# Attention and feed-forward: next keys begun inside the queries, weights loaded over the last tokens, router product on DVE, output stored by GpSimd

## The chip, the cores and the metric

One core of a Trainium2 chip runs the whole program. The metric is the device time of one execution in microseconds (us). Of the kernel before there are three timed executions and one profiled execution; the profile is of one execution alone.

## What is computed

The input is a batch of 4 images, 256 channels of 56 x 56 points, in fp32. Layer 0 is an involution: a group norm, then for each point and each of 32 groups of channels a softmax over a 7 x 7 window, worked out from the window itself, weighs that window; its result is added to the image. Layer 1 takes the 3136 points of an image as tokens of 256 values:

```python
t = _to_tokens(x)
t = t + _L1_attn_ref(_ln_t(t), ...)
t = t + _L1_ffn_ref(_ln_t(t), ...)
x = _from_tokens(t, x)
```

The attention has 8 heads of 32 and no exponential: its weights are a square, divided by their sum over the keys.

```python
scores = jnp.einsum('bnhd,bmhd->bhnm', q, k) * scale
t = jnp.square(scores + C_SHIFT)
attn = t / jnp.sum(t, axis=-1, keepdims=True)
out = jnp.einsum('bhnm,bmhd->bnhd', attn, v).reshape(B, N, D)
return out @ proj_w.T + proj_b
```

The feed-forward works only on the half of the tokens whose router weight is largest, and adds its result, times that weight, to their own rows:

```python
weights = (jnp.einsum('bsd,do->bso', x, wr) + br)[..., 0]
...
_, idx = jax.lax.top_k(weights, k)
sel_idx = idx[:, :kk]
...
h = jax.nn.gelu(jnp.einsum('bkd,dh->bkh', sel, w1) + b1)
y = jnp.einsum('bkh,hd->bkd', h, w2) + b2
...
y = y * w_sel[..., None]
```

## The kernel before

Two functions do the work, one after the other. `conv_layer` computes layer 0 and ends at about 1875 us of the span; the change doesn't touch it. `attn_ffn_layers` (L860) does the rest.

**Attention as sums over pairs.** Since the weights are squares of inner products, the sum over the keys is taken first: for each head, the products of all pairs of the 32 entries of a key, times v, are summed over the tokens, and each query then needs only its own products of pairs. So an image b has two passes, each for two groups g of four heads:

- `keys(b, g)` (L1021) goes over 25 blocks m of 128 tokens. `tokens(m)` issues the projection on PE (matmuls pv) and hands it to ACT and POOL (ls); `features(m)` multiplies the pairs on DVE (phi, 128 x 1920); `add(m, phi)` sums them on PE (accs, accq), one block behind. `coefficients` (L1101) turns the sums into coefficients.
- `queries(b)` (L1222) goes over 7 chunks q of 448 tokens, two groups g and four blocks k of pairs: matmuls pg, a square on ACT (ph), and on PE, one block behind, `add` (acc). After the last block the result is copied by DVE (av).

**Side work.** Everything else is put into a list, `later` (L1416 and on: `aside` at L1473, `run` at L1476). Each entry is a generator; `run` steps the main pass, and after each of its yields `aside` steps every entry once. A yield is therefore a unit of delay, "an aside" below. The side work of the queries is:

- `weigh(b, q, g)` (L1198), the sums by which to divide: matmul pu, on DVE dd, one yield, matmul pn, on DVE dn.
- `divide` (L1279): dn to another layout by four loads on SP (inv), an add and a reciprocal on DVE, a round trip through DRAM on SP (flat, rec), av times rec on DVE; for g = 1 then `tokens_out`.
- `tokens_out(b, q)` (L1313): the output projection on PE (po), added to the tokens on DVE (tk, two buffers), statistics and normalisation on DVE (the rows, which the feed-forward gathers later), uw = rows x router weights and tk + rows on POOL, and two yields later the reduce of uw to w on DVE, and the store of tk into the output on SP.
- `normalise(b + 1, q)` (L975), the layer norm of the next image's tokens, into xn, of which there is one; and `project(b, q + 1)` (L1181), the next chunk's queries (pq).
- `select(b)` (L1376), after the last chunk: the top half of the image's tokens by a search on the bits of w, and then 28 indirect DMAs on POOL, two to a yield, that scatter the rows into `us[b]` in DRAM. For images 0 to 2 it is put into the queries of the next image, for image 3 into the feed-forward.

**The order.** Every instruction of this function is issued through `InOrder` (L841), which keeps each engine's instructions in the order in which the program issues them. So all of them are recorded at L849, and the profile is read by the names of the tiles. An engine whose next instruction waits does nothing else; this holds for the DMA queues of SP and of POOL too.

**The feed-forward** (from L1497) begins after `inner.close()`, which gives back the buffers of the attention, xn among them. Then the loads of w1, w2 (1 MB each) and b2 are issued, and `fetch(0)` and `fetch(1)`, which load rows of `us`. There are 16 parts, four to an image, of 4, 4, 4 and 2 blocks of 112 tokens. For each: `turn` (L1518, transposes ft on PE), `first` (L1532, matmuls ph and a gelu on ACT), `second` (L1551, matmuls py, the rest on DVE (fz, fy), and indirect DMAs on POOL that write the rows into the output), and the `fetch` of the part after next.

The lines on which the side work of an output chunk ends:

```python
gp.tensor_tensor(uw, u, wr.to_broadcast([TB, 4, C]), ALU.mult)
gp.tensor_tensor(tk, tk, u, ALU.add)
yield
yield
w = held["w", b][:, q * 4 : q * 4 + 4]
ve.tensor_reduce(w, uw, AX.X, ALU.add)
...
sy.dma_start(
    out[b, q * CH : (q + 1) * CH].rearrange("(j p) c -> p j c", p=TB), tk
)
```

Of the kernel before, what the change touches and what calls it, by code (L numbers as in the profile page):

```python
# [7 lines left out]
F32 = mybir.dt.float32  # L8
I32 = mybir.dt.int32
AF = mybir.ActivationFunctionType  # L10
ALU = mybir.AluOpType
# [4 lines left out]
P = 128  # L16
NB = 4
C = 256
# [14 lines left out]
FF = 4 * C  # L33
TOPK = int(0.5 * HW) - 1
CH = 8 * W
NCH = HW // CH
NT = (HW + P - 1) // P
TB = 112
NTB = HW // TB
ROW_N = C + 4  # L40
# [821 lines left out]
def attn_ffn_layers(  # L862
# [27 lines left out]
    outp = ctx.enter_context(tc.tile_pool(name="attn_out", bufs=2))  # L890
    tkp = ctx.enter_context(tc.tile_pool(name="tokens", bufs=2))
    slp = ctx.enter_context(tc.tile_pool(name="select", bufs=1))
    mm = ctx.enter_context(tc.tile_pool(name="attn_mm", bufs=2, space=PSUM))
    accp = ctx.enter_context(tc.tile_pool(name="attn_acc", bufs=2, space=PSUM))
    sm = ctx.enter_context(tc.tile_pool(name="attn_sm", bufs=2, space=PSUM))

    inner = ctx.enter_context(ExitStack())
    xnp = inner.enter_context(tc.tile_pool(name="xn", bufs=1))
    kp = inner.enter_context(tc.tile_pool(name="k", bufs=3))
    php = inner.enter_context(tc.tile_pool(name="phi", bufs=2))  # L900
    cp = inner.enter_context(tc.tile_pool(name="coef", bufs=2))
# [2 lines left out]
    ve, te, se, sy, gp = (  # L904
        InOrder(tc, e) for e in (nc.vector, nc.tensor, nc.scalar, nc.sync, nc.gpsimd)
    )
# [35 lines left out]
    p = sm.tile([P, 512], F32, tag="sm", name="pvb")  # L942
# [77 lines left out]

    def keys(b, g):  # L1021

        accs = accp.tile([P, 512], F32, tag="acc", name=f"accs_{b}_{g}")
        accq = accp.tile([P, 512], F32, tag="acc", name=f"accq_{b}_{g}")
        held["sums", b, g] = accs, accq
        vs, ks = {}, {}
        size = lambda m: min(P, HW - m * P)

        def tokens(m):

            mn = size(m)
            if m % 2 == 0:
                held["kv"] = mm.tile([P, 2, 512], F32, tag="mm", name=f"pv_{b}_{g}_{m}")
            p = held["kv"][:mn, m % 2]
            for c in range(2):
                te.matmul(
                    p[:, : 2 * P], xn[:, c, m * P : m * P + mn],
                    wqkv[:, c, C:].rearrange("p (i o) -> p i o", i=2)[:, :, g * P : (g + 1) * P],
                    start=c == 0, stop=c == 1,
                )  # L1040
            k = ks[m] = p[:, :P].rearrange("p (h e) -> p h e", e=DH)
            se.activation(
                lss[m % NKV][:mn, :, HALF : HALF + 2 * DH].rearrange("p h (i e) -> p h i e", i=2),
                k.unsqueeze(2).to_broadcast([mn, 4, 2, DH]), AF.Identity,
            )
            v = vs[m] = kp.tile([P, P], F32, tag="v", name=f"v_{b}_{g}_{m}", bufs=5)
            se.activation(v[:mn], p[:, P : 2 * P], AF.Identity)

        def features(m):

            mn = size(m)
            ls, k = lss[m % NKV], ks.pop(m)
            phi = php.tile([P, 4, NF], F32, tag="phi", name=f"phi_{b}_{g}_{m}")
            mine = ls[:mn, :, HALF : HALF + DH]
            se.activation(phi[:mn, :, :DH], mine, AF.Square)
            ve.tensor_tensor(
                phi[:mn, :, DH:].rearrange("p h (l e) -> p h l e", e=DH),
                k.unsqueeze(2).to_broadcast([mn, 4, HALF - 1, DH]),
                further(ls[:mn, :, HALF + 1 : HALF + 1 + DH], HALF - 1), ALU.mult,
            )  # L1060
            gp.tensor_tensor(
                ls[:mn, :, :HALF], mine[:, :, :HALF], mine[:, :, HALF:], ALU.mult
            )
            return phi

        def add(m, phi):
            mn = size(m)
            v, ls = vs.pop(m), lss[m % NKV]
            first, last = m == 0, m == NT - 1
            for h, r in enumerate(QUARTERS):  # L1070
                te.matmul(accs[r], v[:mn, r], phi[:mn, h], start=first, stop=last)
            for h, r in enumerate(QUARTERS):
                te.matmul(
                    accq[r, :LS], v[:mn, r], ls[:mn, h], start=first, stop=last,
                    skip_group_check=True,
                )

            for h, r in enumerate(QUARTERS):
                k = ls[:mn, h, HALF:]
                te.matmul(  # L1080
                    accq[r, P : P + LS - HALF], k[:, :DH], k, start=False, stop=last,
                    skip_group_check=True,
                )

        tokens(0)
        tokens(1)
        yield
        tokens(2)
        yield
        waiting = None  # L1090
        for m in range(NT):
            phi = features(m)
            if waiting:
                add(*waiting)
            waiting = m, phi
            if m + 3 < NT:
                tokens(m + 3)
            yield
        add(*waiting)
# [98 lines left out]
    def weigh(b, q, g):  # L1198

        gram, line = held["form", b, g]  # L1200
        qT = held["q", b, q][0]
        p = sm.tile([P, 512], F32, tag="sm", name=f"pu_{b}_{q}_{g}")
        te.matmul(
            p[:, :CH], gram, qT[:, g], start=True, stop=True
        )
        dd = qp.tile([P, CH], F32, tag="dd", name=f"dd_{b}_{q}_{g}", bufs=1)
        ve.scalar_tensor_tensor(dd, p[:, :CH], line, qT[:, g], ALU.add, ALU.mult)
        yield

        n = CH // 4  # L1210
        p = sm.tile([P, 512], F32, tag="sm", name=f"pn_{b}_{q}_{g}")
        for j, r in enumerate(QUARTERS):
            te.matmul(
                p[r, :n], heads, dd[:, j * n : (j + 1) * n], start=True, stop=True,
                skip_group_check=True,
            )
        dn = outp.tile([P, n], F32, tag="dn", name=f"dn_{b}_{q}_{g}", bufs=3)
        ve.tensor_copy(dn, p[:, :n])
        held["dn", b, q, g] = dn
        yield  # L1220

    def queries(b):  # L1222
# [26 lines left out]
        for q in range(NCH):  # L1249
            for g in range(2):  # L1250
# [2 lines left out]
                    later.append(normalise(b + 1, q))  # L1253
                if g == 1 and q + 1 < NCH:
                    later.append(project(b, q + 1))
                for k in range(FB):
                    qT = held["q", b, q][0]
                    p = [
# [15 lines left out]
                        add(*waiting)  # L1274
                    waiting = q, g, k, phi
                    yield
        add(*waiting)

    def divide(b, q, g, av):  # L1279
# [33 lines left out]
    def tokens_out(b, q, both):  # L1313

        t = load(b, q, "tr")
        if q == 0:
            held["rows", b] = (slp if b % 2 else xnp).tile(
                [TB, NTB, ROW_N], F32, tag="rows", name=f"rows_{b}"
            )
            held["w", b] = slp.tile([TB, NTB], F32, tag="w", name=f"w_{b}", bufs=2)  # L1320
# [34 lines left out]
        for j in range(4):  # L1355
# [4 lines left out]
        ve.tensor_copy(rows[:, :, C + 2], mv[:, :, 0])  # L1360
        ve.tensor_scalar(rows[:, :, C + 3], dev, 1.0, None, ALU.add)
        uw = tkp.tile([TB, 4, C], F32, tag="uw", name=f"uw_{b}_{q}", bufs=1)
        gp.tensor_tensor(uw, u, wr.to_broadcast([TB, 4, C]), ALU.mult)
        gp.tensor_tensor(tk, tk, u, ALU.add)
        yield
        yield
        w = held["w", b][:, q * 4 : q * 4 + 4]
        ve.tensor_reduce(w, uw, AX.X, ALU.add)
        ve.tensor_scalar(w, w, col("br")[:TB], None, ALU.add)
        sy.dma_start(  # L1370
            out[b, q * CH : (q + 1) * CH].rearrange("(j p) c -> p j c", p=TB), tk
        )
        if q == NCH - 1:
            (later if b == NB - 1 else whole).append(select(b))

# [100 lines left out]
    def run(steps):  # L1476
        for _ in steps:
            aside()
# [3 lines left out]
    for q in range(NCH):  # L1482
        f = slice(q * CH, (q + 1) * CH)
        sy.dma_start(xn[:, :, f], ln0.rearrange("(c p) f -> p c f", p=P)[:, :, f])
    for b in range(NB):
        for g in range(2):
            run(keys(b, g))
            later.append(coefficients(b, g))
            aside()
            if g == 0:  # L1490
                later.append(project(b, 0))
        later.extend(whole)
        whole.clear()
        run(queries(b))

    inner.close()
    fp = ctx.enter_context(tc.tile_pool(name="ffn", bufs=2))  # L1497
    w1 = fp.tile([P, 2, FF], F32, name="w1", bufs=1)
    sy.dma_start(w1, d["ffn_w1"].rearrange("(c p) o -> p c o", p=P))
    w2 = fp.tile([P, FF // P, C], F32, name="w2", bufs=1)  # L1500
    sy.dma_start(w2, d["ffn_w2"].rearrange("(c p) o -> p c o", p=P))
    b2 = fp.tile([TB, 1, C], F32, name="b2", bufs=1)
    sy.dma_start(b2[:, 0], d["ffn_b2"].unsqueeze(0).to_broadcast([TB, C]))

    blocks = (TOPK + TB - 1) // TB
    parts = [(b, m, min(4, blocks - m)) for b in range(NB) for m in range(0, blocks, 4)]

    def fetch(i):


        b, m, k = parts[i]
        rows = fp.tile([TB, 4, ROW_N], F32, tag="rows", name=f"frows_{i}", bufs=3)
        sy.dma_start(
            rows[:, :k], us[b][m * TB : (m + k) * TB].rearrange("(j p) c -> p j c", p=TB)
        )
        held["part", i] = rows

    def turn(i):  # L1518
        k = parts[i][2]
# [64 lines left out]
                )  # L1584
            yield

    fetch(0)
    fetch(1)
    for i in range(len(parts) + 1):
        if i < len(parts):  # L1590
            turn(i)
# [160 lines left out]
```

## Time and profile before

| what | value |
| --- | --- |
| median of three runs | 3934.23 us (3933.35 to 3941.9) |
| the profiled execution's own time | 3942.82 us |
| its span | 3940.7 us |
| mean clock granted to TensorE | 0.959 |
| busy, PE / DVE / ACT / POOL | 3537.7 / 2609.8 / 1945.4 / 1812.5 us |
| start and end of image 0's keys, queries | 1882 - 2040, 2040 - 2263 us |
| image 1 | 2263 - 2430, 2430 - 2704 us |
| image 2 | 2704 - 2860, 2860 - 3142 us |
| image 3 | 3142 - 3290, 3290 - 3514 us |
| feed-forward | 3514 - 3941 us |

How to read it: the page gives each engine's busy time, the span in 40 slices with the busy tenths of each engine, the chain of work that ended last, and groups of instructions by tile. The trace behind it can be asked for waits (which engine waited at which tile for which other engine's tile, how long in total, how often, and the longest) and for a timeline (start, duration, engine, instruction, shapes; in brackets the idle time of the engine just before it and what ended it). A name such as `uw<-rows,awr` is the instruction's output and inputs. DMAs are named in the same way: `us<-rows,to` is a scatter of rows into `us`. A transfer's queue is SPq where SP issued it.

### The profile page before, as it was taken

What the parts mean: (1) busy time and instruction counts of PE and PEld (TensorE: products, weight loads), DVE (VectorE), ACT (ScalarE), POOL (GpSimd) and SP (SyncE); (2) the same over time, 40 slices, a digit from 0 to 9 for tenths busy, and PEclk for the clock granted to TensorE, in tenths of its full rate; (3) what the DMA queues carried; (4) which work ended last, traced back from release to release, by engine and by line L of the source; (5) the groups of instructions that cost most, each with busy time, mean ns of one, the idle gap of its engine ahead of it and who ended that gap; (6) DMA issues with size and microseconds to landing.
All of it is one profiled execution on the core that took longest, in us unless ns stands there. A gap on an engine that the chain in (4) does not pass through costs nothing.

```text
span 3940.7 us, 61459 instructions
## 1 busy us (share of the span) xinstructions
PE 3537.7 (90%) x23248; PEld 1595.4 (40%) x23248; DVE 2609.8 (66%) x3411; ACT 1945.4 (49%) x4093; POOL 1812.5 (46%) x1000
## 2 busy tenths in 40 slices
PE   3989998999799998998899989988897898889998
PEld 1333333333233333332444444334433453336666
DVE  2688888899788988998764486537744585334211
ACT  2767766776477756773245423443243324441111
POOL 1578886889588988997100110132003210311231
PEclk7999999999899999999899999999999999999999
DMA  3666556664656546553102200221012200221110
GB/s 96 155 146 144 126 134 156 144 144 99 146 130 138 125 102 139 120 123 84 50 11 60 60 23 11 57 76 43 1 41 79 55 6 17 64 78 48 37 57 25
DMA packets 337517, 329.97 MB, mean 84 GB/s; under 512 B 68606, under 2 KB 327894, under 8 KB 337222
## 3 DMA queue, kind: packets, MB, share of 16 engines
q1 hardware_dynamic: 322428, 302.52, 33.5%
q0 software_dynamic: 8064, 19.48, 1.6%
q10 hardware_dynamic: 6730, 4.05, 0.4%
q8 instruction: 183, 3.00, 0.3%
q14 instruction: 112, 0.92, 0.1%
HBM read 256.77 MB, written 68.69 MB: 83 GB/s over the span
## 4 chain that ended last, share of the span: by engine, by line
PE 65%; DVE 13%; DMA 12%; issue 4%; POOL 4%; SPq 1%; ACT 1%; ACTq 0%; DVEq 0%; POOLq 0%
PE acc L849 17%; PE p L849 17%; DMA us<-rows,to 6%; PE pv L849 4%; PE accs L849 4%; PE pg L849 4%; PE py L849 4%; DVE pr L849 3%; PE po L849 3%; PE ph L849 3%; PE z L849 3%; DVE phi L849 2%; PE pq L849 2%; DMA xc<-x3d 1%; DVE st L849 1%
## 5 line engine op out<-in xcount | busy, mean ns | idle before, releaser
L849 POOL TENSOR_TENSOR pr<-xc,lg 128x1792 f32<-128x1792 f32 x280 | 1034.3, 3702 | 279.2 <-ACT lg L849 102.6
L849 PE MATMUL acc<-pr,same 128*32 128x448 f32 (+1 forms) x5824 | 677.8, 558 | 71.0 <-DVE pr L849 56.9
L849 PE MATMUL p<-y,cw 128*128 128x400 f32 (+5 forms) x1568 | 682.3, 539 | 2.4 <-ACT y L849 1.5
L849 DVE TENSOR_TENSOR pr<-xc,exp 128x1792 f32<-128x1792 f32 x280 | 559.2, 1997 | 53.6 <-DMA xc<-x3d 29.8
L849 ACT ACTIVATE ph<-pg,unit 128x896 f32<-128x896 f32 x448 | 426.4, 1003 | 291.9 <-PE pg L849 270.7
L849 ACT ACTIVATE y<-p,tb,bn2s 128x200 f32<-128x200 f32 (+1 forms) x728 | 343.8, 522 | 224.5 <-PE p L849 220.6
L849 DVE TENSOR_TENSOR phi<-pv,ls 128x1920 f32<-128x1920 f32 (+1 forms) x200 | 428.6, 2152 | 32.5 <-PE accs L849 21.0
L849 PEld LDWEIGHTS p<-y,cw 128*128 128x128 f32 (+1 forms) x1568 | 266.2, 191 | 400.0 <-issue 200.9
L849 POOL TENSOR_TENSOR uw<-rows,awr 112x1024 f32<-112x1024 f32 x28 | 66.0, 2358 | 665.8 <-DVE rows L849 665.6
L849 DVE TENSOR_TENSOR pr<-xw,exp 128x1792 f32<-128x1792 f32 x168 | 338.2, 2014 | 41.5 <-issue 15.0
L849 POOL TENSOR_TENSOR y<-a,ac 128x896 f32<-128x896 f32 x168 | 276.9, 1649 | 127.0 <-DMA ac<-x3d 95.8
L849 PEld LDWEIGHTS acc<-pr,same 128*32 128x32 f32 (+1 forms) x5824 | 144.6, 110 | 429.9 <-issue 247.7
L849 POOL TENSOR_TENSOR ls<-ls 128x64 f32<-128x64 f32 (+1 forms) x200 | 65.4, 331 | 487.1 <-ACT ls L849 487.1
L849 PE MATMUL pg<-qT,pairs 32*128 32x448 f32 x1792 | 282.3, 605 | 7.1 <-ACT ph L849 6.7
L849 ACT ACTIVATE ls<-pv 128x256 f32<-128x256 f32 (+1 forms) x200 | 77.5, 387 | 414.6 <-PE pv L849 414.6
L849 PE MATMUL pv<-wqkv,xn 128*128 128x256 f32 (+1 forms) x800 | 230.6, 413 | 43.3 <-DVE phi L849 19.7
L849 POOL DMA_INDIRECT us<-rows,to x112 | 107.4, 959 | 304.2 <-DMA us<-rows,to 208.9
L849 PE MATMUL accs<-phi,v 128*32 128x512 f32 (+1 forms) x1600 | 217.1, 614 | 26.5 <-DVE phi L849 23.9
L849 ACT ACTIVATE lg<-p,par 128x448 f32<-128x448 f32 x392 | 233.9, 597 | 4.6 <-PE p L849 4.3
L849 PE MATMUL acc<-ph,cf 128*32 128x448 f32 (+1 forms) x1792 | 218.4, 560 | 0.0
L849 ACT ACTIVATE h<-ph,apar 128x448 f32<-128x448 f32 (+1 forms) x128 | 68.4, 586 | 299.4 <-PE ph L849 298.7
L849 ACT ACTIVATE lg<-lg 128x1120 f32<-128x1120 f32 x168 | 164.1, 1009 | 97.3 <-DVE lg L849 96.8
(247 smaller groups left out, 5311.5 us busy)
## 6 DMA issues: line engine op xcount, KB each, us to landing
xw<-x3d SPq DMA_DIRECT2D x224, 248.0 KB
xq<-in_x SPq DMA_DIRECT2D x47, 448.0 KB
xc<-x3d SPq DMA_DIRECT2D x54, 248.0 KB
xc<-x3d SPq DMA_DIRECT2D x54, 247.0 KB
xc<-x3d SPq DMA_DIRECT2D x54, 246.0 KB
xc<-x3d SPq DMA_DIRECT2D x54, 245.0 KB
xr<-in_x SPq DMA_DIRECT2D x224, 56.0 KB
xs<-xr SPq DMA_DIRECT2D x224, 56.0 KB
```

What stands on the lines that cost most here:

```text
L849: return lambda *a, **k: self.tc.keep_in_program_order(of(*a, **k))
```

## The change

Six edits, all in `attn_ffn_layers`:

- **Router product.** uw is computed by DVE (`ve`) in place of POOL (`gp`).
- **Output store.** tk is stored by a DMA that GpSimd issues right after its own tk + rows, in place of one that SP issued two yields later; one of the two yields ahead of the reduce of uw is gone.
- **weigh** has one more yield between dd and pn.
- **Keys.** In `queries(b)` the first step of `keys(b + 1, 0)` is taken ahead of the last `add`: with it the first three `tokens` are issued, without yields between them (before, two yields lay there). The two sums of the keys are allocated when their first product is added.
- **Weights and rows early.** `beforehand()` issues the loads of w1, w2 and the fetches of parts 0 and 1 as side work of the last chunk of the last image, in its first group (b = 3, q = 6, g = 0). For that, w1 and w2 lie in the buffer of xn, which image 3's queries no longer read, and so do two of the three places for fetched rows; the third is allocated after `inner.close()`.
- **Pools.** xn moves to a pool that isn't closed with the attention; the rows of the even images get a pool of their own.

```diff
--- before.py
+++ after.py
@@ -890,12 +890,13 @@
     outp = ctx.enter_context(tc.tile_pool(name="attn_out", bufs=2))
     tkp = ctx.enter_context(tc.tile_pool(name="tokens", bufs=2))
     slp = ctx.enter_context(tc.tile_pool(name="select", bufs=1))
+    xnp = ctx.enter_context(tc.tile_pool(name="xn", bufs=1))
     mm = ctx.enter_context(tc.tile_pool(name="attn_mm", bufs=2, space=PSUM))
     accp = ctx.enter_context(tc.tile_pool(name="attn_acc", bufs=2, space=PSUM))
     sm = ctx.enter_context(tc.tile_pool(name="attn_sm", bufs=2, space=PSUM))
 
     inner = ctx.enter_context(ExitStack())
-    xnp = inner.enter_context(tc.tile_pool(name="xn", bufs=1))
+    rowp = inner.enter_context(tc.tile_pool(name="rows", bufs=1))
     kp = inner.enter_context(tc.tile_pool(name="k", bufs=3))
     php = inner.enter_context(tc.tile_pool(name="phi", bufs=2))
     cp = inner.enter_context(tc.tile_pool(name="coef", bufs=2))
@@ -1020,9 +1021,6 @@
 
     def keys(b, g):
 
-        accs = accp.tile([P, 512], F32, tag="acc", name=f"accs_{b}_{g}")
-        accq = accp.tile([P, 512], F32, tag="acc", name=f"accq_{b}_{g}")
-        held["sums", b, g] = accs, accq
         vs, ks = {}, {}
         size = lambda m: min(P, HW - m * P)
 
@@ -1067,6 +1065,11 @@
             mn = size(m)
             v, ls = vs.pop(m), lss[m % NKV]
             first, last = m == 0, m == NT - 1
+            if first:
+                held["sums", b, g] = [
+                    accp.tile([P, 512], F32, tag="acc", name=f"acc{i}_{b}_{g}") for i in "sq"
+                ]
+            accs, accq = held["sums", b, g]
             for h, r in enumerate(QUARTERS):
                 te.matmul(accs[r], v[:mn, r], phi[:mn, h], start=first, stop=last)
             for h, r in enumerate(QUARTERS):
@@ -1082,11 +1085,8 @@
                     skip_group_check=True,
                 )
 
-        tokens(0)
-        tokens(1)
-        yield
-        tokens(2)
-        yield
+        for m in range(3):
+            tokens(m)
         waiting = None
         for m in range(NT):
             phi = features(m)
@@ -1206,6 +1206,7 @@
         dd = qp.tile([P, CH], F32, tag="dd", name=f"dd_{b}_{q}_{g}", bufs=1)
         ve.scalar_tensor_tensor(dd, p[:, :CH], line, qT[:, g], ALU.add, ALU.mult)
         yield
+        yield
 
         n = CH // 4
         p = sm.tile([P, 512], F32, tag="sm", name=f"pn_{b}_{q}_{g}")
@@ -1253,6 +1254,8 @@
                     later.append(normalise(b + 1, q))
                 if g == 1 and q + 1 < NCH:
                     later.append(project(b, q + 1))
+                if g == 0 and (b, q) == (NB - 1, NCH - 1):
+                    later.append(beforehand())
                 for k in range(FB):
                     qT = held["q", b, q][0]
                     p = [
@@ -1274,6 +1277,10 @@
                         add(*waiting)
                     waiting = q, g, k, phi
                     yield
+
+        if b + 1 < NB:
+            held["keys"] = keys(b + 1, 0)
+            next(held["keys"])
         add(*waiting)
 
     def divide(b, q, g, av):
@@ -1314,7 +1321,7 @@
 
         t = load(b, q, "tr")
         if q == 0:
-            held["rows", b] = (slp if b % 2 else xnp).tile(
+            held["rows", b] = (slp if b % 2 else rowp).tile(
                 [TB, NTB, ROW_N], F32, tag="rows", name=f"rows_{b}"
             )
             held["w", b] = slp.tile([TB, NTB], F32, tag="w", name=f"w_{b}", bufs=2)
@@ -1360,16 +1367,15 @@
         ve.tensor_copy(rows[:, :, C + 2], mv[:, :, 0])
         ve.tensor_scalar(rows[:, :, C + 3], dev, 1.0, None, ALU.add)
         uw = tkp.tile([TB, 4, C], F32, tag="uw", name=f"uw_{b}_{q}", bufs=1)
-        gp.tensor_tensor(uw, u, wr.to_broadcast([TB, 4, C]), ALU.mult)
+        ve.tensor_tensor(uw, u, wr.to_broadcast([TB, 4, C]), ALU.mult)
         gp.tensor_tensor(tk, tk, u, ALU.add)
-        yield
+        gp.dma_start(
+            out[b, q * CH : (q + 1) * CH].rearrange("(j p) c -> p j c", p=TB), tk
+        )
         yield
         w = held["w", b][:, q * 4 : q * 4 + 4]
         ve.tensor_reduce(w, uw, AX.X, ALU.add)
         ve.tensor_scalar(w, w, col("br")[:TB], None, ALU.add)
-        sy.dma_start(
-            out[b, q * CH : (q + 1) * CH].rearrange("(j p) c -> p j c", p=TB), tk
-        )
         if q == NCH - 1:
             (later if b == NB - 1 else whole).append(select(b))
 
@@ -1482,9 +1488,38 @@
     for q in range(NCH):
         f = slice(q * CH, (q + 1) * CH)
         sy.dma_start(xn[:, :, f], ln0.rearrange("(c p) f -> p c f", p=P)[:, :, f])
+    blocks = (TOPK + TB - 1) // TB
+    parts = [(b, m, min(4, blocks - m)) for b in range(NB) for m in range(0, blocks, 4)]
+
+    def fetch(i):
+
+
+        b, m, k = parts[i]
+        rows = places[i % 3]
+        sy.dma_start(
+            rows[:, :k], us[b][m * TB : (m + k) * TB].rearrange("(j p) c -> p j c", p=TB)
+        )
+        held["part", i] = rows
+
+
+    w1, w2 = (
+        xn[:, i, : 2 * FF].rearrange("p (k o) -> p k o", o=o) for i, o in enumerate((FF, C))
+    )
+    places = [
+        xn[:TB, i, 2 * FF : 2 * FF + 4 * ROW_N].rearrange("p (j c) -> p j c", j=4)
+        for i in range(2)
+    ]
+
+    def beforehand():
+        sy.dma_start(w1, d["ffn_w1"].rearrange("(c p) o -> p c o", p=P))
+        sy.dma_start(w2, d["ffn_w2"].rearrange("(c p) o -> p c o", p=P))
+        fetch(0)
+        fetch(1)
+        yield
+
     for b in range(NB):
         for g in range(2):
-            run(keys(b, g))
+            run(keys(b, g) if b == 0 or g else held.pop("keys"))
             later.append(coefficients(b, g))
             aside()
             if g == 0:
@@ -1495,25 +1530,9 @@
 
     inner.close()
     fp = ctx.enter_context(tc.tile_pool(name="ffn", bufs=2))
-    w1 = fp.tile([P, 2, FF], F32, name="w1", bufs=1)
-    sy.dma_start(w1, d["ffn_w1"].rearrange("(c p) o -> p c o", p=P))
-    w2 = fp.tile([P, FF // P, C], F32, name="w2", bufs=1)
-    sy.dma_start(w2, d["ffn_w2"].rearrange("(c p) o -> p c o", p=P))
+    places.append(fp.tile([TB, 4, ROW_N], F32, name="frows", bufs=1))
     b2 = fp.tile([TB, 1, C], F32, name="b2", bufs=1)
     sy.dma_start(b2[:, 0], d["ffn_b2"].unsqueeze(0).to_broadcast([TB, C]))
-
-    blocks = (TOPK + TB - 1) // TB
-    parts = [(b, m, min(4, blocks - m)) for b in range(NB) for m in range(0, blocks, 4)]
-
-    def fetch(i):
-
-
-        b, m, k = parts[i]
-        rows = fp.tile([TB, 4, ROW_N], F32, tag="rows", name=f"frows_{i}", bufs=3)
-        sy.dma_start(
-            rows[:, :k], us[b][m * TB : (m + k) * TB].rearrange("(j p) c -> p j c", p=TB)
-        )
-        held["part", i] = rows
 
     def turn(i):
         k = parts[i][2]
@@ -1584,8 +1603,6 @@
                 )
             yield
 
-    fetch(0)
-    fetch(1)
     for i in range(len(parts) + 1):
         if i < len(parts):
             turn(i)
```

## The prediction

> **What bounds the kernel now.** I read the page first (engine totals, slices, the chain that ended last), then the waits, then the timelines around the longest waits.
>
> ```profile
> PE 3537.7 (90%) x23248; PEld 1595.4 (40%) x23248; DVE 2609.8 (66%) x3411; ACT 1945.4 (49%) x4093; POOL 1812.5 (46%) x1000
> PE   3989998999799998998899989988897898889998
> PE 65%; DVE 13%; DMA 12%; issue 4%; POOL 4%; SPq 1%; ACT 1%; ACTq 0%; DVEq 0%; POOLq 0%
> ```
>
> PE is busy for 90% of the span and is most of the chain. The diff adds and removes no matmul, so the change can win only PE's idle time; from about 1875 us on (attention and feed-forward, the only part it touches) the slices 7 and 8 show where some is. The waits of PE, then of DVE, from there on (releaser; total us, count, longest us):
>
> ```profile
> PE pn L849 <- DVE dd L849: 70.7, 25, 16.1
> PE accs L849 <- DVE phi L849: 23.9, 26, 2.0
> PE ft L849 <- DMA frows<-us: 20.5, 2, 12.2
> DVE w L849 <- POOL uw L849: 47.7, 6, 16.7
> ```
>
> The largest item is pn waiting for DVE's dd: 25 waits. Three of them are long (14.2, 14.1, 16.1 us, one in each of images 1, 2, 3), the other 22 take 26.3 together, 1.2 each. In image 1 the long one looks like this on PE, on DVE and on POOL (start, duration, instruction, [idle before it <- releaser]):
>
> ```profile
> 2589.19 0.96 PE L849 MATMUL acc<-ph,cf 128*32 128x448 f32 x8
> 2604.34 0.60 PE L849 MATMUL pn<-dd,heads 128*32 128x112 f32 x8 [14.19 <-DVE dd L849]
> 2604.93 3.09 PE L849 MATMUL pq<-xn,wqkv 128*128 128x448 f32 x4
> ```
> ```profile
> 2601.41 1.22 DVE L849 TENSOR_REDUCE w<-uw 112x4 f32<-112x1024 f32 x1 [14.71 <-POOL uw L849]
> 2602.67 1.04 DVE L849 TENSOR_SCALAR w<-w,apar 112x4 f32<-112x4 f32 x1
> 2603.62 0.67 DVE L849 SCALAR_TENSOR_TENSOR dd<-pu,line,qT 128x448 f32<-128x448 f32 x1
> ```
> ```profile
> 2598.07 0.94 POOL L849 DMA_INDIRECT us<-rows,to  x1 [1.92 <-DMA us<-rows,to]
> 2599.03 2.35 POOL L849 TENSOR_TENSOR uw<-rows,awr 112x1024 f32<-112x1024 f32 x1
> 2601.33 2.34 POOL L849 TENSOR_TENSOR tk<-tk,rows 112x1024 f32<-112x1024 f32 x1
> ```
>
> Read from the bottom: POOL's 28 scatters of the previous image go out 2.84 us apart, each waiting for the one before; uw, the router product, stands behind those already queued. DVE works in order: its w reduce waits 14.7 us for uw, dd stands behind w, and PE's pn behind dd. The matmul after it takes 3.09 us where it usually takes 1.67: the clock fell during the idle time.
>
> The feed-forward's start and the one large gap inside it:
>
> ```profile
> 3513.06 0.92 PE L849 MATMUL acc<-qT,cd 128*128 128x448 f32 x2
> 3526.14 1.73 PE L849 MATMUL ft<-aident,frows 112*128 112x112 f32 x8 [12.17 <-DMA frows<-us]
> 3806.70 0.98 PE L849 MATMUL ft<-aident,frows 112*128 112x112 f32 x4 [8.36 <-DMA frows<-us]
> ```
>
> The first is the loading of weights and rows, which isn't issued before the pools of attention close (SP issues w at 3514.05).
>
> **What the Trainium skill says.** "TensorE: Matmul & The Clock Gate", part 1: after some 3.4 us of idleness the clock halves, and some 3.4 us of work restore it. The trace agrees: 3.09 against 1.67 us above, and the first 32 matmuls of the feed-forward take 14.04 us against 12.19 later. "SBUF — State Buffer", "Who interferes with whom": DVE and GpSimd share a port as a lock that the loser waits for. The trace agrees; a DVE add on 14 elements, 0.16 us elsewhere, sits out a POOL product:
>
> ```profile
> 2171.32 2.34 POOL L849 TENSOR_TENSOR uw<-rows,awr 112x1024 f32<-112x1024 f32 x1 [29.90 <-DVE rows L849]
> 2171.56 2.14 DVE L849 TENSOR_SCALAR inv<-inv 128x14 f32<-128x14 f32 x1
> 2178.35 0.62 DVE L849 COPY av<-acc 128x448 f32<-128x448 f32 x1 [4.38 <-PE acc L849]
> ```
>
> "DMA: Bandwidth & Descriptors", "Anatomy of one DMA — SWDGE (gpsimd) path": about 2.0 us plus bytes over 436e3 per us; for an output store of 448 KB an estimate of 3.05 us to landing. No plain GpSimd store is in this trace.
>
> **The change, part by part.** The profiled run took 3942.8 us (span 3940.7, 2.1 around it), 8.6 above the median of 3934.2; I take the sum off the first and carry the difference over to the median.
>
> *a. uw on DVE.* 28 products leave POOL (2.36 us each, 66 in all). On DVE I price one at 1.22 us, an estimate from the formula in "VectorE: DVE Perf Modes", the errata section, (1024+151)/0.96 ns; it gives 1.09 for the 896-element product of the normalisation, which the trace has at 1.08. 28 x 1.22 = 34 us on DVE. In the queries DVE still idles 4.4 to 6.3 us in each of the 14 rounds of an image (4.38 in the last line above), so even a product stretched to 3.6 by the lock (1.22 + tk add's 2.35) is hidden; without that cover it would cost 34. w no longer waits for POOL, so the three stalls go: -44.4. What is late next: tk add and the store behind it stay on POOL after the scatters, and DVE's next but one tk (two buffers) needs them 27 us later or more; they are 15 late. That holds. The clock after each stall (3.09 against 1.67, and a little on the matmuls after it) is some 2 us: -6. Together **-50**.
>
> *b. One more yield in weigh.* pn is issued one aside (about 3 us of PE work) after dd; the 22 ordinary waits of 1.2 lie under that. Who waits for pn is dn and the inverse, several asides later. **-24** of 26.3 (bounds -20 and -26).
>
> *c. Weights and rows early.* beforehand() puts w1 and w2 (1 MB each) and two fetches (466 KB each) on SP's queue as the last chunk of queries begins (3487): 3.03 MB at the 269 GB/s that the DMA view shows for 3514 to 3527 are 11 us, ahead of 3514. Removed: 12.2 idle, 1.9 of cold clock. Moved past: the four inv loads, the flat/rec round trip and tr of the last two divisions stand behind these 3 MB. DVE's inv add may be 8 us late, of which it idles about 6 anyway; then rec, av and the last po come late: +3 (0 to +10). tr's own wait at the start (2.6) goes, since other work precedes it. **-14**.
>
> *d. The gap at 3806.* The fetch waits for feed-forward scatters that stand on POOL behind the last image's 28. Those begin one aside (about 3 us) earlier, so four in place of two fit into POOL's 9 idle us before 3714: some 5.7 us less, and part of the 2.5 of cold clock behind it (16.48 against 13.98 on py). **-7** (0 to -11).
>
> *e. Next keys begun inside the queries, and the keys stage.* PE's gaps at a boundary are 0.70 + 0.70 + 0.62 + 2.46 us, three boundaries: -13 at most, and about 1 us at each of the four changes of g. Against it: in the keys DVE (phi 2.15 per token block) is nearly level with PE (about 2.3), and the products of q=5 and 6 (2 x 1.22 at three boundaries, up to 3.6 each under the lock) and the stores' time on POOL beside ls come in there; the side work loses two asides for each keys stage, so the last divisions end later. I take **+5** (-5 to +18).
>
> *f. Output store on GpSimd.* POOL's time for one isn't in the trace. Below: 0.94 us, what the indirect DMA of 112 rows takes. Above: four times that, 3.8, for 448 rows. It waits only for tk add, ahead of it on POOL; behind it stand the scatters and, in the keys, ls. 28 x 3.8 = 106 us on an engine that is 46% busy and that nothing but tk waits for: 0 in the queries, its share in the keys is in e. SP loses its wait for tk (in image 1 its out store waited for POOL from 2583.8 to 2603.7, with inv and tr loads behind it): a gain contained in a.
>
> Sum: -50 -24 -14 -7 +5 = **-90**. 3942.8 - 90 = 3852.8; against the median 3934.2 - 90 = 3844, say **3845**.
>
> **Rivals.** (1) *The burst of loads costs what it saves*: the last inv loads wait for 3 MB and po waits for them. For it: SP's one queue in front of a short tail. c falls to 0: 3845 + 14 = 3859. (2) *The stall only changes its name*: the tk buffer, released by tk add and store behind the scatters, becomes DVE's wait, or phi in the keys waits for DVE and ls for stores. Against: 27 us of slack for 15. A store at 12 us would use it up; half of a comes back, and e at its upper end: 3845 + 25 + 13 = 3883. (3) *Slower: a GpSimd store that holds POOL long.* In images 1 to 3 the queries take 260 us on average (274, 282, 224), in which POOL has 28 x 2.84 = 80 us of scatters and 7 x 2.35 of tk adds, 96 together: seven stores fit if each takes under (260-96)/7 = 23 us. The 90 are lost where 3 x (7S + 96 - 260) = 90, S = 28 us; at 30 us the time is 3934 - 90 + 138 = 3982. Against: 28 us is over seven times my upper bound from the indirect DMA. (4) *More than the sum*: e at -5, the clock restored in full: 3845 - 10 - 8 = 3827.
>
> **How the numbers follow.** Forecast 0.55; (1) 0.20; (2) 0.11; (3) 0.04; (4) 0.10. The range reaches from (4), less a few us, to (2): 3822 to 3886. A measurement of this kernel can tell about 0.2% (8 us) from no change. Faster: all but (3), less a little for cases that add up: 0.94; same 0.02; slower 0.04.
>
> **What would show it.** Right: no DVE wait of w on POOL, and pn's wait on dd near zero in the list; a uw row on DVE near 1.22 us; ft's first wait gone; the weights' loads before 3514; POOL's store rows between 0.9 and 3.8 us. Wrong: tk<-po on DVE waiting for a store; av waiting for rec at the end of image 3 by about 10 us; accs waiting for phi by more than 24 + 18 us; the gap at 3806 still 8 us.

## The result and the profile after

The changed kernel takes 3898.59 us (median of 7), the kernel before 3940.93 beside it: a ratio of 0.9897, interval 0.9876 to 0.9918. That is 41 us faster where 90 were forecast, and 13 us beyond the upper end of the range, 3886. The profiled spans say the same: 3940.7 before, 3896.8 after. First the page's engine totals and its chain, then some of PE's waits from 1860 us on (releaser; total us, count, longest us), of the changed kernel:

```profile
PE 3531.0 (91%) x23248; PEld 1595.5 (41%) x23248; DVE 2638.3 (68%) x3439; ACT 1940.0 (50%) x4093; POOL 1789.5 (46%) x1000
PE 72%; DVE 13%; DMA 8%; issue 3%; POOL 2%; SPq 1%; ACT 1%; ACTq 0%; DVEq 0%; POOLq 0%
```
```profile
PE pv L849 <- DVE phi L849: 38.9, 30, 2.1
PE accs L849 <- DVE phi L849: 32.2, 32, 3.7
PE mean L849 <- DMA t<-xs: 24.4, 13, 3.2
...
PE po L849 <- DMA tr<-xs: 8.7, 6, 2.9
...
PE mean L849 <- DVE dd L849: 6.9, 3, 2.8
PE po L849 <- DVE av L849: 3.8, 1, 3.8
...
PE ft L849 <- DMA xn<-us: 3.6, 1, 3.6
```

pn's 70.7 us on dd, the item at the head of the old list, is gone, and w no longer stands among DVE's waits. Three items have grown: the waits for phi in the keys by 28 us (19.7 on pv and 23.9 on accs before), mean waiting for the load of t by 22 (2.6 before), and po and mean waiting for tr and for DVE by some 18.

The scatter stretch of image 1, on DVE and on POOL, shows the mechanism of step a at work:

```profile
2584.84 1.22 DVE L849 TENSOR_TENSOR uw<-rows,awr 112x1024 f32<-112x1024 f32 x1
2586.42 1.21 DVE L849 TENSOR_REDUCE w<-uw 112x4 f32<-112x1024 f32 x1
```
```profile
2607.08 2.36 POOL L849 TENSOR_TENSOR tk<-tk,rows 112x1024 f32<-112x1024 f32 x1
2609.74 0.76 POOL L849 DMA_DIRECT2D out<-tk  x1 [0.30 <-POOL tk L849]
```

tk's add is 21 us behind uw, held up by the scatters, and nobody waits for it: DVE starts each of its 56 tk<-po within 0.1 us of po's end. The store costs POOL 0.76 us.

I cut the traces at the first accs of each keys pass and the first acc of each queries pass. Lengths in us; the last two columns are experiments below, `a_latekeys` and `best1`.

| stage | before | after | late keys | best |
| --- | --- | --- | --- | --- |
| image 0 keys / queries | 137.5 / 240.7 | 136.7 / 243.0 | 137.7 / 244.0 | 136.6 / 237.8 |
| image 1 | 152.2 / 273.8 | 163.0 / 259.1 | 155.4 / 257.9 | 154.7 / 252.0 |
| image 2 | 152.5 / 273.0 | 162.2 / 254.3 | 155.8 / 253.4 | 153.6 / 252.8 |
| image 3 | 150.8 / 254.3 | 162.2 / 226.9 | 155.6 / 227.3 | 156.7 / 227.5 |
| feed-forward | 404.0 | 394.1 | 393.6 | 395.2 |

From before to after the queries give 58 us (the wait ahead of the feed-forward counts as image 3's), the feed-forward 10, and the keys of images 1 to 3 take 32 back. (The end of the convolution, whose code no run touches, differs by up to 12 us between the profiles, so stages are compared, not spans; each length is of one execution.) The rows for image 1's keys, before and after (window, length, busy PE, PEld, DVE, ACT, POOL, clock, DMA share, GB/s):

```profile
2269.60:2421.80 152.20, 130.69 (x1463) 71.70 (x1463) 127.00 (x125) 38.85 (x147) 25.17 (x53) 0.96 0.05 15
```
```profile
2265.40:2428.40 163.00, 134.80 (x1466) 72.43 (x1466) 135.34 (x139) 38.84 (x146) 23.13 (x50) 0.93 0.05 14
```

The same matmuls keep PE busy 4 us longer at a lower clock, and DVE has 8 us more to do. About half of these 8 stays when the keys start late (131.5 in `a_latekeys`): the two products, 2.4, and an inv add stretched from 0.2 to 2.3. The rest is side work of the last chunks (statistics, a part of the normalisation, av), which the earlier start has moved over from the queries.

### The profile page after: what moved, and what is told of

Read it like the earlier page. It is cut to its first block, busy times and chain, and to the rows that moved or that the text cites. A ratio compares the mean times of both kernels' runs of the same rounds, so it can differ in the third digit from the quotient of the medians.

```text
span 3896.8 us, 61488 instructions
## 1 busy us (share of the span) xinstructions
PE 3531.0 (91%) x23248; PEld 1595.5 (41%) x23248; DVE 2638.3 (68%) x3439; ACT 1940.0 (50%) x4093; POOL 1789.5 (46%) x1000
## 4 chain that ended last, share of the span: by engine, by line
PE 72%; DVE 13%; DMA 8%; issue 3%; POOL 2%; SPq 1%; ACT 1%; ACTq 0%; DVEq 0%; POOLq 0%
PE acc L849 18%; PE p L849 17%; PE py L849 5%; PE pg L849 5%; PE pv L849 5%; PE ph L849 4%; PE po L849 4%; PE accs L849 4%; DVE phi L849 3%; DVE pr L849 3%; PE z L849 3%; PE pq L849 2%; SPq L849 1%; DMA t<-xs 1%; DMA xc<-x3d 1%
## 5 line engine op out<-in xcount | busy, mean ns | idle before, releaser
L849 DVE TENSOR_TENSOR phi<-pv,ls 128x1920 f32<-128x1920 f32 (+1 forms) x200 | 428.2, 2152 | 43.3 <-PE accs L849 24.9
L849 POOL TENSOR_TENSOR tk<-tk,rows 112x1024 f32<-112x1024 f32 x28 | 86.0, 3073 | 628.0 <-DVE rows L849 627.8
L849 PE MATMUL accs<-phi,v 128*32 128x512 f32 (+1 forms) x1600 | 220.6, 623 | 34.2 <-DVE phi L849 32.2
```

The lines of the kernel that those rows point to most:

```text
L849: return lambda *a, **k: self.tc.keep_in_program_order(of(*a, **k))
```

## The experiments

My theory after the result: the long stalls went as forecast, but pn's ordinary waits had covered the load of t, and the keys, where DVE is nearly level with PE, took part of the gain back. The rivals: one of the parts, the GpSimd store above all, costs what others win; or step a alone earned less than thought. Ratios are to the kernel before, with 95% intervals; 0.001 is 4 us.

### Which part moves the three long stalls

**Router product on DVE alone** (`b_uw`).

```diff
-        gp.tensor_tensor(uw, u, wr.to_broadcast([TB, 4, C]), ALU.mult)
+        ve.tensor_tensor(uw, u, wr.to_broadcast([TB, 4, C]), ALU.mult)
```

> The kernel before with the router product on DVE alone. The prediction's step a: the three long waits of pn go, -44 and -6 of cold clock, about 3890. Theory after the result (part of the gain is given back in the keys, where DVE sets the pace): the three waits go in the queries, and each of the keys stages of images 1 to 3 grows by 4 to 7 us, about 3906. If the keys grow for another reason (order, store), they stay at 151 to 153 us here.

Measured: 1.0007 (0.9995 to 1.0018): nothing. The keys grow by 4.8, 8.0 and 6.3 us, as my theory has it, but both times were wrong: the queries of images 1 to 3 are shorter by only 17 us in all. w's long waits are gone and pn's fall by 44, but po now waits 30 us more for tr. SP, then PE, in image 1:

```profile
2595.09 0.34 SPq L849 DMA_DIRECT2D out<-tk  x1
2595.47 2.55 SPq L849 DMA_DIRECT2D inv<-dn  x4
2598.12 0.40 SPq L849 DMA_DIRECT2D tr<-xs  x1
```
```profile
2601.78 1.20 PE L849 MATMUL po<-aident,tr 128*112 128x128 f32 x4 [8.11 <-DMA tr<-xs]
```

The store stands on SP's queue until POOL, behind its scatters, has added tk (at 2595.07); inv and tr stand behind the store, and po waits for tr. The stall has a second path, which takes back two thirds of what the first gave.

What the product does to the keys is seen at the start of image 1's, before on PE, then here on DVE and PE:

```profile
2273.41 2.05 PE L849 MATMUL pv<-wqkv,xn 128*128 128x256 f32 x4 [2.46 <-DVE inv L849]
```
```profile
2266.23 2.31 DVE L849 TENSOR_SCALAR inv<-inv 128x14 f32<-128x14 f32 x1
2270.75 2.04 PE L849 MATMUL pv<-wqkv,xn 128*128 128x256 f32 x4 [5.75 <-DVE inv L849]
```

uw (1.22 us) and an inv add of 2.31 in place of 0.17 now stand ahead of phi on DVE, and PE's wait grows from 2.46 to 5.75 us, in each of images 1 to 3.

**Output store on SP again, in the changed kernel** (`a_spstore`).

```diff
-        gp.dma_start(
-            out[b, q * CH : (q + 1) * CH].rearrange("(j p) c -> p j c", p=TB), tk
-        )
         yield
 ...
         ve.tensor_scalar(w, w, col("br")[:TB], None, ALU.add)
+        sy.dma_start(
+            out[b, q * CH : (q + 1) * CH].rearrange("(j p) c -> p j c", p=TB), tk
+        )
```

> The changed kernel with the output's store on SP after the reduce again (the one yield stays). Theory store (GpSimd's store delays ls or blocks DVE's port in the keys): keys 4 us shorter each, about 3886. Theory without it: no gain, and up to 10 us more, since SP's queue waits behind it for tk again, 3898 to 3908.

Measured: 1.0017 (1.0008 to 1.0026), some 47 us more than the changed kernel: with this one part undone, the whole gain is gone. The queries of images 1 to 3 are longer by 13.5, 16.6 and 21.1 us. Image 1, on SP, DVE and PE:

```profile
2593.74 0.34 SPq L849 DMA_DIRECT2D out<-tk  x1
```
```profile
2601.51 0.62 DVE L849 TENSOR_TENSOR av<-av,rec 128x448 f32<-128x448 f32 x1 [17.69 <-DMA rec<-flat]
```
```profile
2602.19 1.19 PE L849 MATMUL po<-wo,av 128*112 128x256 f32 x2 [13.07 <-DVE av L849]
```

This is the second path with the first one open. It isn't quite the old place: the store stands on SP's queue a yield earlier than in the kernel before, and SP waits for tk 233.8 us in all (86.2 before, 43.3 in `b_uw`), so 47 us is the price of this placing. That the GpSimd store makes the keys long falls too: they are 161 here, 162 with it.

**Store on GpSimd without the product** (`b_store`), and **both** (`b_uw_store`): the kernel before with the change's edits to the end of `tokens_out`, in the first case with uw left on POOL.

```diff
         gp.tensor_tensor(tk, tk, u, ALU.add)
+        gp.dma_start(
+            out[b, q * CH : (q + 1) * CH].rearrange("(j p) c -> p j c", p=TB), tk
+        )
         yield
-        yield
 ...
-        sy.dma_start(
-            out[b, q * CH : (q + 1) * CH].rearrange("(j p) c -> p j c", p=TB), tk
-        )
```

> The kernel before with the output's store on GpSimd right after tk's add, and one yield less ahead of the reduce; the router product stays on POOL. Theory two locks (the scatters hold the queries back by two paths, DVE's w behind uw and SP's loads behind the store's wait for tk; each alone is enough): w still waits, so no gain, 3935 to 3945. Theory store alone (SP's wait was the whole stall): the 44 us and their cold clock go, about 3895.

> The kernel before with the router product on DVE and the output's store on GpSimd, nothing else. Theory two locks: the three long stalls go for good in each of images 1 to 3, -50, less 12 to 16 for the product in the keys: about 3906. If the gain of the changed kernel hangs on another of its edits: 3930 or more.

Measured: store alone 1.0093 (1.0076 to 1.011), 37 us slower; both 0.9916 (0.9901 to 0.9932), 33 us faster. In the first the long stalls stay, and w's reduce, which comes a yield earlier, waits longer for uw than before (47.7 us, 6 times):

```profile
DVE w L849 <- POOL uw L849: 102.0, 17, 26.6
```

That alone isn't the loss: pn's wait for dd grows by only 5 us, to 75.7. In the profiled execution 24 us of the loss lie in the keys of images 1 to 3, where PE idles no longer than before (21.0 and 21.5 us in image 1) but is busy 138.3 us in place of 130.7 at a clock of 0.91; why the clock is lower there wasn't found. With both, pn waits 25.9 us in all, only the ordinary 1.2 each, and the queries of images 1 to 3 are shorter by 12.8, 15.5 and 18.4, and their keys longer by 3.5, 3.1 and 5.1. Two locks on one door: nothing, a loss, and 33 us when both are opened.

### What the ordinary waits of pn were worth

**One more yield in weigh alone** (`b_yield`), and **with the product** (`b_uw_yield`).

```diff
         ve.scalar_tensor_tensor(dd, p[:, :CH], line, qT[:, g], ALU.add, ALU.mult)
         yield
+        yield
```

> The kernel before with one more yield in weigh alone. The prediction's step b: the 22 waits of 1.2 us go, and the three long ones shrink by an aside each (about 9 us in all), about 3908. Theory after the result: in images 0 to 2 the normalisation's mean then waits for its load t (1.5 us, about 15 times), because pn's wait had covered that load; the gain is 5 to 18 us, about 3928.

> The kernel before with both. The prediction's a and b together: -74, about 3867. Theory after the result: no wait of pn on dd, but 20 us of mean on t, and 12 to 20 us more in the keys, about 3900. Keys stages of images 1 to 3 near 157 us each if DVE's product is the cause, near 152 if not.

Measured: 0.996 (0.9945 to 0.9975), 16 us, and 0.9971 (0.9961 to 0.9981), 11 us. In the first, the long stalls only move to the next matmul (pq waits 42.5 us for dd, most of it in three stalls). Image 0, which has none, is the clean reading: pn's 6.3 us go, mean's wait for t rises from 0.4 to 8.3, and its queries stay at 240.4 (240.7). The 16 us come from the queries of images 1 to 3, which are 15 shorter: 7 of idle time, and 8 of busy time over the same matmuls. The second runs into SP's path as `b_uw` did; the forecast's 3867 and my 3900 are both far off. Against `b_uw` alone the yield brings it some 14.

How pn's wait covered the load is seen in image 0. Before (PE; SP issued this load of t at 2128.59), then after (the load at 2122.70):

```profile
2131.88 0.40 PE L849 MATMUL pn<-dd,heads 128*32 128x112 f32 x8 [1.27 <-DVE dd L849]
2132.21 1.77 PE L849 MATMUL mean<-t,amean 128*128 128x448 f32 x4
```
```profile
2126.39 1.74 PE L849 MATMUL mean<-t,amean 128*128 128x448 f32 x4 [1.67 <-DMA t<-xs]
```

3.6 and 3.7 us from issue to use: mean starts at the same distance from the load, and the yield has only changed which matmul does the waiting.

**One more yield behind the load of t, in the changed kernel** (`a_t`).

```diff
         t = load(b, q, "t")
         yield
+        yield
```

> The changed kernel with one more yield between the load of t and the mean in normalise. If t's load is what mean waits for and nothing stands behind it: the 24 us of mean on t go, about 3876. Rival: the wait moves one place on (var, tr or the rows' norm), gain under 6 us, about 3894.

Measured: 0.9857 (0.9834 to 0.9879), 3886.71 us, 12 less. mean's waits fall from 24.4 to about 3, and var's for sq come to 9.0, so half of the wait comes out as time: between the two theories. PE idles 20 us less in the queries, but is busy 12 us longer; why wasn't found.

### Where the keys' 32 us come from

**Keys after the last add** (`a_latekeys`): the early step out, the two yields back.

```diff
-        for m in range(3):
-            tokens(m)
+        tokens(0)
+        tokens(1)
+        yield
+        tokens(2)
+        yield
 ...
-        if b + 1 < NB:
-            held["keys"] = keys(b + 1, 0)
-            next(held["keys"])
         add(*waiting)
 ...
-            run(keys(b, g) if b == 0 or g else held.pop("keys"))
+            run(keys(b, g))
```

> The changed kernel without the early keys: keys begin after the last add again, with the two yields. Theory order (the early start puts phi ahead of the last divisions on DVE and takes asides away, so that the keys lengthen): about 6 us less in each of three images, about 3881. Theory DVE (the product and its lock lengthen the keys, the early start gains a little): 3 to 5 us more per boundary, about 3909.

**The two halves apart**: only the yields back (`a_early_yields`), only the early step out (`a_late_noyields`).

> The changed kernel with the two yields in keys put back, and the first step (now two token blocks) still ahead of the last add. If the lost asides are the cause of the longer keys: about 17 us less than the changed kernel, 3880. If the start ahead of the last add is: no change, 3895 to 3900, keys stages at 162.

> The changed kernel with the keys begun after the last add, and still without the two yields. If the early start is the cause: about 3880, keys stages at 155. If the lost asides are: 3895 to 3900.

Measured: 0.9848 (0.9829 to 0.9868), 3881.77 us, for the whole; 0.9889 (0.9868 to 0.991), 3898.25, with only the yields back; 0.9851 (0.9829 to 0.9872), 3884.17, with only the early step out. By the times, the start ahead of the last add costs 14 to 17 us, and the yields nothing that can be told. By the stages, the two look alike: the keys are 159.2, 161.7 and 158.8 us with only the early step out (not 155, as expected) and 158.5, 162.2 and 158.9 with only the yields back, some 8 less in all either way, and 20 less with both. So the keys need both halves, and where the time of each half goes isn't settled. In the trace of the changed kernel, DVE at the boundary first waits 2.5 us for ACT's v ahead of phi, then 2.5 us for the last acc ahead of av, with the next phi behind it. Some 17 us later PE runs dry. DVE, POOL and PE there:

```profile
2277.01 1.22 DVE L849 TENSOR_TENSOR uw<-rows,awr 112x1024 f32<-112x1024 f32 x1
2278.14 2.32 DVE L849 TENSOR_SCALAR inv<-inv 128x14 f32<-128x14 f32 x1
2280.37 2.15 DVE L849 TENSOR_TENSOR phi<-pv,ls 128x1920 f32<-128x1920 f32 x1
```
```profile
2277.03 3.40 POOL L849 TENSOR_TENSOR tk<-tk,rows 112x1024 f32<-112x1024 f32 x1 [13.25 <-DVE rows L849]
```
```profile
2282.66 1.94 PE L849 MATMUL accs<-phi,v 128*32 128x512 f32 x8 [3.72 <-DVE phi L849]
```

3.72 us without work, and accs takes 1.94 in place of 1.06. The lines show the product and the stretched inv right ahead of this phi, so the product has a share in this stall too. With late keys image 1's keys lose 2.0 of their 28.2 idle us, and 5.6 of PE's busy time: that is most of the 7.6 between 163.0 and 155.4. In all three images it is 6 idle and 14 busy. That split isn't firm: image 2's keys keep PE busy 136.0 us in `b_uw` and 129.5 in `b_uw_store`, with the same DVE work (131.5 and 131.4). Nor is it the one long wait that costs the clock, for with late keys PE waits 5.75 us near the start of each of these keys passes. Why the late order is kinder to the clock stays open.

**Product of chunks 5 and 6 on POOL** (`a_pool`), the rest as changed.

```diff
-        ve.tensor_tensor(uw, u, wr.to_broadcast([TB, 4, C]), ALU.mult)
+        (gp if q >= NCH - 2 and b + 1 < NB else ve).tensor_tensor(uw, u, wr.to_broadcast([TB, 4, C]), ALU.mult)
```

> The changed kernel with the router product of chunks 5 and 6 of images 0 to 2, those that fall into the next keys, on POOL again. Theory DVE: each product is 1.2 us and some lock on the engine that sets the pace there; six of them, -8 to -15, about 3887. Theory order: no change within 3 us.

Measured: 0.986 (0.9837 to 0.9883), 3884.55 us. The keys of images 1 to 3 are shorter by 4.7, 1.7 and 1.2 only; accs waits 10 us less for phi, and accq waits 17 us more for ls, which stands behind the product on POOL. The rest of the 14 us is spread over the other stages, some of which the edit doesn't touch, so I take 8 from the keys and no more.

### Weights and rows early

`a_nobefore` calls `beforehand()` after `inner.close()`; `a_c` takes the buffers there as well, as the kernel before does.

> The changed kernel with the loads of w1, w2 and the first two parts' rows issued after the attention's pools have closed, as before. The prediction's c: 14 us more. From the trace of the changed kernel: the wait of 12.2 us comes back with about 2 us of cold clock, but po's waits for av (3.8) and tr (2.9) beside the loads go; about 7 us more, 3906.

> The changed kernel with the feed-forward's weights and fetched rows in buffers taken after the attention's close, as before, and loads there (the run a_nobefore left the buffers in place, and its loads came no later). The prediction's c: 14 us more; from the traces: ft's wait of 12.2 and 2 of cold clock come back, po's 3.8 and 2.9 in front of it go: 8 to 14 us more than the changed kernel, 3905 to 3912.

Measured: 0.9871 (0.9853 to 0.989), 3894.0 us, and 0.9931 (0.9915 to 0.9947), 3912.12. With the early call undone no time is lost: SP loads w1 and w2 at 3408.61, far ahead of their place in the program and earlier than in the changed kernel (3456.49). So not every load keeps its place on SP's queue, as the description of the kernel before has it; that these could move because their part of xn was free is likely, but wasn't tried. It is the place in xn that wins. With the buffers as before, ft waits 12.1 us at the start and 8.3 at the later gap, and the time is 13.5 longer.

The traces show what the place does to the later gap. It stood ahead of the last part of image 2, which has two blocks. Before, its fetch goes out at 3803.79, when all four output scatters of the part that had the buffer have landed, the last issued at 3801.12; in `a_c` it is the same (3768.1 and 3770.8). In the changed kernel it goes out after the second of the four, those of the two blocks that it overwrites. POOL, then SP:

```profile
3754.61 0.93 POOL L849 DMA_INDIRECT out<-fy,frows  x1 [4.66 <-issue]
```
```profile
3757.28 0.30 SPq L849 DMA_DIRECT2D frows<-us  x1
```

The other two follow at 3760.10 and 3764.67, and this part's ft waits for nothing. The 3.6 us in the list above are a new wait, of the part after it.

### All together

`best1`: the changed kernel with late keys, the later mean, and six products on POOL. `a_t_latekeys`: without the last. `best2`: `best1` without the early call of `beforehand()`.

> The changed kernel with three of its costs taken back at once: keys begin after the last add, the product of chunks 5 and 6 of images 0 to 2 on POOL, one more yield behind the load of t. If the three are independent: 12 to 17 for each of the first and third, 5 more for the product, about 3862. If the first two are one and the same wait on DVE: about 3870.

> The changed kernel with late keys (yields in place) and one more yield behind the load of t; the product stays on DVE throughout. If the two losses are independent: 12 and 17 less than the changed kernel, about 3868, level with the version that also has six products on POOL; if the product matters beside late keys, 3872 to 3876.

> The version with late keys, the later mean and six products on POOL (3868), with beforehand() called after the attention's close; the buffers stay in xn, so the loads may still go early. If the burst ahead of the last inv loads costs 4 us, about 3864; if not, 3868.

Measured: 0.982 (0.9805 to 0.9836), 3867.62 us; 0.9828 (0.9805 to 0.9851), 3874.97; 0.9817 (0.9795 to 0.9838), 3871.56. The first two losses add up within the intervals (24 us together, 12 and 17 apart); what the products on POOL and the later call of `beforehand()` bring on top can't be told from nothing. The best version is 31 us ahead of the changed kernel and 71 ahead of the one before.

## Why the prediction was wrong

Two steps failed: e, whose term was far too small, and b, which counted waits as gains that others took over. The other parts fell short by less.

- **a, right in sum, wrong in what carries it.** The three stalls of 44.4 us are gone, and with both locks open the queries of images 1 to 3 are 47 us shorter, of 50 forecast. The working gave them to the product and called SP's wait for tk "a gain contained in a". It is a second lock: the product alone gives 1.0007, the store alone 1.0093, both 0.9916. uw takes 1.22 us, as priced.
- **b, failed in part: the step that all 22 waits "lie under that".** It asked who waits for pn, and not what else had been landing during pn's wait. In images 0 to 2 mean now waits for t, 3.7 us after its issue: 22 us of new wait against 26 of old. Only image 3, which normalises nothing, loses its few for good. Where runs single the yield out it brings 16 and 14 us of the 24, more than these waits alone would give.
- **c and d, about two thirds.** Forecast 21 together, 13.5 measured; by the stages of `a_c`, some 6 for c and 9 for d. The wait of 12.2 is gone, but po's waits for av (3.8) and tr (2.9) stand in its place, about twice the +3 that the step foresaw. d came near its 7 by luck. Its reason was the scatters' earlier start; `a_c` keeps that, and its gap is 8.3 us again. What closes the gap is the buffer, as the traces above show.
- **e, failed, by the size of the term: +5 against +32.** The range was -5 to +18. The early start was booked as a gain of up to 13 and costs 14 to 17. The product on DVE makes the keys 12 us longer (`b_uw_store`) or 19 (`b_uw`) where it comes without the early start; of its cost beside the early start, 8 come back with six products on POOL. Late keys take 20 back. Much of this is PE's busy time at a lower clock. The step knew that DVE is nearly level with PE there and still took +5; the clock's fall after idle time, which the working priced for the stalls, it left out for this stage. Why the clock suffers more in one order than in another stays open.
- **f, right.** 0.75 us of POOL per store, below my lower bound of 0.94. Rival (3) needed 28.
- Of the missing 49 us, e explains some 27, b 8 to 10, c and d 7, a 3. The times behind these figures carry some 10 us of uncertainty each, so that they add up so closely is in part luck. Rival (2) was the right kind of doubt: half of it, phi in the keys, came true, by 28 us, where its sum had 18 at most for e. The sign that it named, accs waiting over 42, missed it (32.2), since most of the growth came on pv. On tk, its other half, nothing waited, and t it didn't name.

## What to carry to other kernels

When an in-order engine is late, follow every queue that holds its result: a stall with two paths of like length shows one of them in the waits, and removing either alone gives nothing. Before you book an ordinary wait as a gain, look which loads land during it and by how much. And work started early on an engine that is nearly the bottleneck needn't be a gain: here it moved side work of DVE into the stage where DVE is level with PE, and cost 14 to 17 us.

## What the runs showed of the hardware

- A GpSimd store of 448 KB takes 0.75 us of POOL and lands 3.8 us after its issue, against the estimate of 3.05 from "DMA: Bandwidth & Descriptors".
- The shared port makes POOL the loser as well: tk's add, which takes 2.35 us alone, takes 3.40 beside DVE's uw (in 19 of 28 cases), and DVE's small inv behind it 2.32 in place of 0.17 ("SBUF — State Buffer", "Who interferes with whom"). uw itself takes 1.22 in all 28.
- A half clock can follow waits well under the 3.4 us of "TensorE: Matmul & The Clock Gate". In image 1's keys of the changed kernel pv takes 2.07 us in place of 1.13 after a wait of 1.91, with waits of 1.50 and 0.37 shortly before it; in image 2's, accs stays at 1.06 after a wait of 2.29. So the length of one wait doesn't tell:

```profile
2319.00 2.07 PE L849 MATMUL pv<-wqkv,xn 128*128 128x256 f32 x4 [1.91 <-DVE phi L849]
```
